# Cross-attention on one core: one weight quarter kept in SBUF, values loaded quad by quad, and one output product moved behind the values

## The chip, the cores and the metric

One core of one Trainium2 chip. The metric is the device time of one execution in microseconds (us), lower is better. The kernel before was timed in three runs.

## The reference

The inputs are `x` (8 batches x 256 rows x 1024), a context of the same shape that serves as keys and as values, a mask over the 256 context rows, two 1024 x 1024 weights and the layer norm's gamma and beta. All is fp32.

```python
xn = layernorm(x) * gamma + beta
Q = heads(xn @ Wq.T)                     # 32 heads of 32
scores = Q @ K.T / sqrt(32)              # K = V = heads(context)
attn = softmax(where(mask, scores, -inf)) @ V
out = x + merge(attn) @ Wout.T
```

## The kernel before

**Tiles.** The work goes by quads of four heads. A batch has 8 quads, so there are N = 64 quads, and one loop over n = 0..63 issues one slot each. Batch b's quads are 8b to 8b+7. The order on every engine is the order in which the program issues; no scheduler moves anything.

**One slot.** In slot n TensorE (PE) gets, in this order: the scores of quad n+1 (`sc`, L479), project steps of place 0, the values of quad n-2 (`pv`, L622, softmax times V), project steps of place 1, a query product or `make_q`, project steps of place 2. The other engines get the softmax of quad n+1: VectorE (DVE) adds the mask and takes the minimum (L515), ScalarE (ACT) takes the exponentials (L519), GpSimd (POOL) normalizes (L528), DVE transposes blocks into `pT` (L534), ACT puts a part aside in `pc` (`aside`, L540). The `tail` of a softmax, on SyncE's (SP's) queue, issues two pT-to-pT copies (L600), then the list `between` of loads, then two pc-to-pT copies (L604). For quads 0 to 7 and 57 to 62 the tail is put off to the next slot. A list `ahead` of loads is issued just before the tail. `pT` has three buffers, `pc` (pool `asp`) three.

**Query projection.** Batches 0 to 2 use whole weights (`make_q`). From batch 3 (`SPLIT`) on, the product of two 2x2 block matrices is made from seven half-size products, one per slot, in slots 8(b-1)+2 to 8(b-1)+8, in the order S1, S4, A11, S2, S3, A22, A12 (`Q_PRODUCTS`). Their PSUM bank is `ps_q` (one buffer, tag `pq`). Weight quarters and their sums lie in the tile `wq`, at the places of `W_AT`. Three of them share one SBUF tile, `ring`: T1 (for S1), B11 (for A11) and T3 (for S3) are kept in DRAM (`keep_wq`) and loaded back by halves of 512 KB (`load_ring`) in every batch. T4 lies in `wq` where B11 was before.

**Output projection.** Of a batch b it also takes seven products of four steps each (`PRODUCTS`: A11, A12, S2, S3, A22, S1, S4), spread over slots 8(b+1) to 8(b+1)+8 by the table `STEPS`, with (k0, k1, k2) steps at places 0, 1, 2. A step is one 128x512 matmul, two PE records. Their bank is `ps_o` (one buffer, tag `po`). A11 opens the bank in slot 8b+9 at place 0; `keep_p1` (ACT, L702) copies the result P1 aside; A12 then adds to the same bank from place 2 of that slot on, so that the bank holds P1 + A12 B21, which `store` (DVE, L736) adds to the residual `r` and sends out. `add_p1` (POOL, L727) adds P1 to the other three residual quarters. `ENDS` is the table of batch 6; batch 7 is written out after the loop.

**Values.** `load_v` loads V for a pair of quads (512 KB, two buffers) in the list `between` of every odd slot. `load_k` does so for keys in even slots.

**SP's queue** is one queue in order for all these DMAs: k, v, x, r, ring, output weights `wo`, the copies of pT and pc, the 64 KB copies `xnT<-xe` of a transposed x (`move_x`, L327), and the stores.

Of the kernel before, what the change touches and what calls it, by code (L numbers as in the profile page):

```python
# [46 lines left out]
F32 = mybir.dt.float32  # L47
# [4 lines left out]
P = 128  # L52
# [7 lines left out]
def xattn_kernel(  # L60
# [11 lines left out]
    nc = tc.nc  # L72
    B, S, D = x.shape
    T = mask.shape[2]
    HD = D // HEADS
# [6 lines left out]
    K = 32  # L82
    NA = P // K
    NI = T // (2 * K)
    assert NH == 4 and NS == 2 and NT == 2 and S == 256 and T == 256 and NA == 4
    NEG_SCALE = -1.0 / math.sqrt(HD)
    N = B * NQ

    const = ctx.enter_context(tc.tile_pool(name="const", bufs=1))
# [4 lines left out]
    vp = ctx.enter_context(tc.tile_pool(name="vp", bufs=2))  # L94
    atp = ctx.enter_context(tc.tile_pool(name="atp", bufs=3))
    ep = ctx.enter_context(tc.tile_pool(name="ep", bufs=4))
    ptp = ctx.enter_context(tc.tile_pool(name="ptp", bufs=3))
    asp = ctx.enter_context(tc.tile_pool(name="asp", bufs=3))
    up = ctx.enter_context(tc.tile_pool(name="up", bufs=1))
    sm = ctx.enter_context(tc.tile_pool(name="sm", bufs=8))  # L100
    dram = ctx.enter_context(tc.tile_pool(name="dram", bufs=1, space=bass.MemoryType.DRAM))
# [3 lines left out]
    ps_q = ctx.enter_context(tc.tile_pool(name="ps_q", bufs=1, space=PS))  # L105
    ps_o = ctx.enter_context(tc.tile_pool(name="ps_o", bufs=1, space=PS))

    NK = D // P // 2
    ring = const.tile([P, NK, NK, P], F32, tag="ring", name="ring")
# [13 lines left out]
    xs, ks, vs, rs = {}, {}, {}, {}  # L123
# [8 lines left out]
    def load_k(n):  # L132

        b, g = divmod(n, NQ)
        ks[n] = kp.tile([P, 2, T], F32, tag="k", name=f"k_{n}")
        nc.sync.dma_start(
            ks[n], kv[b, g // 2, :, : 2 * T].rearrange("p (g t) -> p g t", g=2)
        )

    def load_v(n):  # L140

        b, g = divmod(n, NQ)
        vs[n] = vp.tile([P, NI, 2 * P], F32, tag="v", name=f"v_{n}")
        nc.sync.dma_start(
            vs[n], kv[b, g // 2, :, 2 * T :].rearrange("p (i v) -> p i v", i=NI)
        )

    def load_res(b, s, h):
# [8 lines left out]
    sums_x = const.tile([P, 2, NK, NA, K], F32, tag="sx", name="sx")  # L157
    kept = {
        name: dram.tile([P, NK, NK * P], F32, tag=name, name=f"kept_{name}")
        for name in ("T1", "B11", "T3")  # L160
    }
    wo = const.tile([P, 7, NK, 512], F32, tag="wo", name="wo")
    B11, B21, B22, T1, T2, T3, T4 = range(7)
    B12 = T1

    def load_wq(o):
        nc.sync.dma_start(wq[:, o], wq_[o])
# [36 lines left out]
    for o in range(2, 5):  # L204
        load_wq(o)
    load_k(2)
    load_v(0)
    for o in range(5, 8):
        load_wq(o)

# [148 lines left out]
    def fold(o):  # L359
# [13 lines left out]
    SPLIT = 3  # L373
    SOON, LATE = 0, NK
    W_AT = {"B12": (SOON, 0), "B22": (SOON, NK), "B11": (LATE, 0), "B21": (LATE, NK),
            "T2": (SOON, 0), "T3": (SOON, 0), "T4": (LATE, 0)}

    def weights(name, o):

        if name == "ring":  # L380
            return ring[:, o]
        first, k = W_AT[name]
        return wq[:, first + o, ds(k, NK)]

# [20 lines left out]
    def load_ring(name, half):  # L405
# [1 line left out]
        nc.sync.dma_start(ring[:, pair].rearrange("p o c q -> p o (c q)"), kept[name][:, pair])  # L407

    Q_PRODUCTS = (
        ("S1", "ring", True), ("S4", "B22", False), ("A11", "ring", True), ("S2", "T2", False),  # L410
        ("S3", "ring", False), ("A22", "T4", False), ("A12", "B21", True),
    )

# [50 lines left out]
    mbs, scs, pTs, pvs, ats, pos = {}, {}, {}, {}, {}, {}  # L464
# [19 lines left out]
    def softmax(*args):  # L484
        for _ in softmax_parts(*args):
            pass
# [127 lines left out]
    def values(n):  # L614
        pvs[n] = [
            ps_v.tile([P, 2, NS, K], F32, tag="pv", name=f"pv_{n}_{r}") for r in range(2)
        ]
        pT = pTs.pop(n)
        for i in range(NI):
            for j in range(NH):  # L620
                for r in range(2):
                    nc.tensor.matmul(  # L622
                        pvs[n][r][j * HD : (j + 1) * HD],
                        vs[n - n % 2][ts(r, 2 * K), i, ds(n % 2 * P + j * HD, HD)],
                        pT[ts(r, 2 * K), :, i, j, :, :],
                        start=(i == 0), stop=(i == NI - 1),
                    )

    def copy_at(n):
# [4 lines left out]
        for r, pv in enumerate(pvs.pop(n)):  # L634
# [12 lines left out]
    PRODUCTS = (  # L647
        ("A11", B11, True), ("A12", B21, False), ("S2", T2, True), ("S3", T3, False),
        ("A22", T4, False), ("S1", T1, True), ("S4", B22, False),
    )  # L650

    STEPS = ((0, 0, 0), (4, 0, 3), (0, 1, 2), (0, 2, 2), (0, 2, 1), (0, 1, 2), (0, 0, 3), (0, 1, 2),
             (0, 2, 0))
    ENDS = ((0, 0, 2), (0, 0, 5), (0, 0, 5)) + ((0, 0, 4),) * 4 + ((0, 0, 0),)
    ENDS_TO = {2: (0, 0), 3: (0, 1), 4: (1, 1), 5: (1, 0), 6: (1, 1), 7: (0, 1)}
    assert all(sum(map(sum, one)) == len(PRODUCTS) * NK for one in (STEPS, ENDS))

    def operand(b, name):  # L660

        if name in ("S2", "S1"):
            return s2s[b]
        s, k = {"A11": (0, 0), "A12": (0, 1), "A21": (1, 0), "A22": (1, 1),
                "S3": (1, 0), "S4": (0, 1)}[name]
        return ats[b, k][:, :, s].rearrange("p c a k -> p c (a k)")
# [9 lines left out]
            operand(b, name)[:, c], operand(b, one)[:, c], operand(b, two)[:, c], op  # L676
        )

    s2s, p1s = {}, {}

    def product_steps(b, steps):
        for step in steps:
            p, c = divmod(step, NK)
            name, which, begins = PRODUCTS[p]
            po = pos.get(b)
            if b == B - 2 and name in ("A12", "S2"):

                begins = name == "A12"
                if begins and c == 0:
                    po_q[0] = ps_q.tile([P, 512], F32, tag="pq", name=f"po_{b}_{name}")  # L690
                po = po_q[0] if begins else po
            elif begins and c == 0:
                po = pos[b] = ps_o.tile([P, 512], F32, tag="po", name=f"po_{b}_{name}")
            nc.tensor.matmul(  # L694
                po, operand(b, name)[:, c], wo[:, which, c],
                start=begins and c == 0, stop=c == NK - 1,
                skip_group_check=not begins,
            )

    def keep_p1(b):  # L700
        p1s[b] = up.tile([P, 512], F32, tag="p1", name=f"p1_{b}")
        nc.scalar.copy(p1s[b], pos[b])  # L702


    po_q, ends_kept = [None], {}
# [76 lines left out]
    firsts = {NQ * (b - 1) + 2: b for b in range(SPLIT, B)}  # L782
# [55 lines left out]

    away, rings = {n: [] for n in range(N)}, {n: [] for n in range(N)}
    for n, name, half in (  # L840
        (9, "B11", 0), (10, "B11", 1), (15, "T1", 0), (16, "T1", 1), (17, "T3", 0), (19, "T3", 1),
    ):
        away[n].append(partial(keep_wq, name, half))
    for n, b in firsts.items():
        for slots, name in (((n - 3, n - 2), "T1"), ((n, n), "B11"), ((n + 2, n + 2), "T3")):
            if b > SPLIT or name != "T1":
                for half, slot in enumerate(slots):
                    rings[slot].append(partial(load_ring, name, half))
# [34 lines left out]
    steps, evacuations = {}, {n: [] for n in range(N + 1)}  # L883
    for b in range(B - 1):
        done, ends = 0, b == B - 2
        for i, counts in enumerate(ENDS if ends else STEPS):
            n = NQ * (b + 1) + i
            for place, k in enumerate(counts):
                steps.setdefault((n, place), []).append((b, range(done, done + k)))
                done += k  # L890
        for i, *what in (
            ((2, keep_p1), (3, take_po_q), *((i, copy_po, i) for i in range(3, 8))) if ends else
            ((1, keep_p1), (2, store, 0, 0), (3, take, 0, 1), (4, take, 1, 1), (6, store, 1, 0),
             (7, store, 1, 1), (8, store, 0, 1))
        ):
            evacuations[NQ * (b + 1) + i].append((what[0], b, *what[1:]))

    def project_steps(n, place):
        for one in steps.get((n, place), ()):
            product_steps(*one)  # L900


    for n in range(N):
        b, i = divmod(n - NQ, NQ)
        new_q = new_qs[n]
        between = []
        if n % 2 and n + 1 < N:
            between.append(partial(load_v, n + 1))
        elif n % 2 == 0 and n + 4 < N:
            between.append(partial(load_k, n + 4))  # L910
        ahead = rings[n]
        if n + 3 in firsts or n + 2 in firsts:
            between, ahead = between + ahead, []
        if b >= 0:
            if b == B - 2 and i - 1 in (5, 6):
                between.append(partial(send, b, *ENDS_TO[i - 1]))
# [18 lines left out]
        for what, one, *args in evacuations[n]:  # L935
            if one == B - 2:
                now.append(partial(what, one, *args))
            else:
                place = "p1" if what is keep_p1 else "soon" if i == 2 else 0 if i in (3, 4, 6) else 1
                hooks.setdefault(place, []).append(partial(what, one, *args))  # L940
        if n >= 2:
            values(n - 2)
# [20 lines left out]
        if n + 1 < N:  # L963
            softmax(n + 1, copies, ahead, between, hooks, fill)
        else:
            copy_at(n - 2)
            for load in between:
                load()
        if b >= 0 and i == 1:
            sum_at(b, "S2", *((slice(NK - 1, NK),) if b == B - 2 else ()))  # L970
# [42 lines left out]
        if N - NQ + 2 < n < N - 1:  # L1013

            c = n - (N - NQ + 3)
# [58 lines left out]
    for cols in (first_cols, last_cols):  # L1074
        po = to_c12[:, cols] if cols.start == 0 else ps_v.tile([P, P], F32, tag="pv", name="po_end")
# [43 lines left out]
```

## Time and profile before

| | |
|---|---|
| timed runs | 575.7 us median (574.19, 575.7, 576.84) |
| the profiled execution | span 577.6 us from first to last instruction; no other time is recorded for it |
| granted TensorE clock | 0.997 of full, mean |
| busy | PE 567.7 us (98%), DVE 458.6 (79%), ACT 412.1 (71%), POOL 404.7 (70%) |
| DMA | 117.98 MB, mean 204 GB/s |
| chain that ended last | PE 79%, POOL 8%, DVE 6%, issue 2%, DMA 2%, ACT 1% |

A slot lasts 7.5 us in the first batch and 8.5 to 9.4 us later. A row of the timeline gives the start, the duration, the engine, the line, the operation, the tiles, the shape, the number of merged instructions, and in brackets the idle time before it with what ended that. A PE row's duration overlaps the next row's start by some 0.07 us, so that costs are best read from one start to the next.

### The profile page before, as it was taken

The numbers are of one execution on the slowest core, as the hardware profiler recorded it, in microseconds if no ns is written. First come the engines' busy times: TensorE is split into PE (matmuls) and PEld (weight loads), VectorE is DVE, ScalarE is ACT, GpSimd is POOL, SyncE is SP. The second block draws the span as 40 slices with busy tenths as digits, with TensorE's granted clock in tenths as the row PEclk, the third lists the DMA queues.
The fourth block names the chain that finished last, engine by engine and source line by source line (L and its number), as shares of the span: only waits on it lengthen the run. The fifth ranks groups of instructions, "written<-read, shape, count | busy, mean of one in ns | idle before, by whom it ended". The sixth has DMA issues, their size and how long they took to land.

```text
span 577.6 us, 20001 instructions
## 1 busy us (share of the span) xinstructions
PE 567.7 (98%) x7162; PEld 392.2 (68%) x7162; DVE 458.6 (79%) x1695; ACT 412.1 (71%) x1425; POOL 404.7 (70%) x672
## 2 busy tenths in 40 slices
PE   8999998999999999899999999999999999999998
PEld 8788884666667777477776677667766777755444
DVE  6897887687878878678888888888877868879823
ACT  4688886677758857678577976779767866869820
POOL 1788998699896896665657775676656667448780
PEclk9999999999999999999999999999999999999999
DMA  8675778756778667776686767887658865436741
GB/s 312 224 211 184 218 240 209 244 172 196 196 229 271 215 188 219 225 222 202 181 247 181 233 196 201 237 257 217 186 160 254 239 192 147 130 112 182 214 154 74
DMA packets 47475, 117.98 MB, mean 204 GB/s; under 512 B 9104, under 2 KB 9872, under 8 KB 47376
## 3 DMA queue, kind: packets, MB, share of 16 engines
q1 hardware_dynamic: 47088, 116.69, 68.2%
q8 instruction: 57, 0.93, 0.7%
q14 instruction: 42, 0.34, 0.2%
q10 hardware_dynamic: 288, 0.01, 0.0%
HBM read 65.28 MB, written 11.53 MB: 133 GB/s over the span
## 4 chain that ended last, share of the span: by engine, by line
PE 79%; POOL 8%; DVE 6%; issue 2%; DMA 2%; ACT 1%; SPq 0%; DVEq 0%; POOLq 0%; ACTq 0%
PE po_S L694 17%; PE pq_A L440 16%; PE sc L479 10%; PE po_A L694 10%; PE pv L622 9%; PE pq_S L440 6%; POOL e L528 6%; PE pq L340 6%; DVE e L515 3%; PE po_end L761 2%; DVE pT L534 1%; PE po_last L761 1%; POOL wo L183 1%; DMA pT<-pT 1%; ACT e L519 1%
## 5 line engine op out<-in xcount | busy, mean ns | idle before, releaser
L528 POOL TENSOR_SCALAR e<-e,rden 128x256 f32<-128x256 f32 x512 | 237.0, 483 | 131.1 <-DVE rden L526 129.6
L519 ACT ACTIVATE e<-e,mn 128x256 f32<-128x256 f32 x512 | 254.0, 500 | 53.8 <-DVE mn L515 53.8
L534 DVE STREAM_TRANSPOSE pT<-e 128x512 f32<-128x512 f32 x256 | 180.7, 707 | 54.8 <-POOL e L528 43.8
L515 DVE CUSTOM_DVE_ANT_0 e<-sc,mb 128x256 f32<-128x256 f32 x512 | 185.9, 416 | 23.7 <-PE sc L479 23.2
L540 ACT COPY pc<-pT 128x512 f32<-128x512 f32 x128 | 79.0, 617 | 72.0 <-DVE pT L534 43.0
L519 ACT ACTIVATION_READ_ACCUMULATOR e<-e,mn 128x1 f32 x512 | 97.7, 191 | 0.0
L340 PE MATMUL pq<-xnT,wq 128*128 128x256 f32 (+1 forms) x368 | 84.1, 383 | 0.0
L340 PEld LDWEIGHTS pq<-xnT,wq 128*128 128x128 f32 x368 | 68.7, 190 | 14.3 <-issue 3.9
L479 PEld LDWEIGHTS sc<-k,qa 32*128 32x128 f32 x1024 | 46.2, 184 | 42.4 <-issue 20.6
L694 PE MATMUL po_S<-wo,at 128*128 128x512 f32 x152 | 74.5, 607 | 0.3 <-DVE r L736 0.3
L622 PE MATMUL pv<-pT,v 64*32 64x128 f32 x4096 | 74.3, 274 | 0.0
L622 PEld LDWEIGHTS pv<-pT,v 64*32 64x32 f32 x4096 | 56.9, 105 | 25.3 <-issue 11.9
L479 PE MATMUL sc<-k,qa 32*128 32x256 f32 x1024 | 73.6, 400 | 0.1
L694 PE MATMUL po_A<-wo,at 128*128 128x512 f32 x128 | 61.9, 616 | 4.2 <-issue 2.2
L694 PE MATMUL po_S<-wo,s 128*128 128x512 f32 x104 | 50.2, 606 | 0.3 <-DVE r L736 0.3
L515 DVE DVE_READ_ACCUMULATOR2_ANT mn<- 128x1 f32 x512 | 42.6, 83 | 0.0
L694 PEld LDWEIGHTS po_A<-wo,at 128*128 128x128 f32 x128 | 22.6, 190 | 29.2 <-issue 23.4
L526 DVE RECIPROCAL rden<-den 128x2 f32<-128x2 f32 x256 | 37.5, 146 | 5.9 <-ACT e L519 4.6
L440 PEld LDWEIGHTS pq_A<-xnT,wq 128*128 128x128 f32 x320 | 37.3, 192 | 4.8 <-issue 4.1
L694 PEld LDWEIGHTS po_S<-wo,at 128*128 128x128 f32 x152 | 25.6, 190 | 20.8 <-issue 19.3
L440 PE MATMUL pq_A<-xnT,wq 128*128 128x128 f32 x320 | 37.3, 275 | 0.0
L635 ACT COPY at<-pv 128x128 f32<-128x128 f32 x128 | 26.2, 253 | 8.7 <-PE pv L622 8.7
(95 smaller groups left out, 605.3 us busy)
## 6 DMA issues: line engine op xcount, KB each, us to landing
v<-in_kv_dram SPq DMA_DIRECT2D x32, 512.0 KB, 4.2
pT<-pT SPq DMA_DIRECT2D x128, 128.0 KB, 2.9
pT<-pc SPq DMA_DIRECT2D x128, 128.0 KB, 4.7
ring<-kept_T SPq DMA_DIRECT2D x18, 512.0 KB, 5.8
k<-in_kv_dram SPq DMA_DIRECT2D x32, 256.0 KB, 3.0
x<-in_x_dram SPq DMA_DIRECT2D x14, 512.0 KB, 5.5
r<-in_x_dram SPq DMA_DIRECT2D x28, 256.0 KB, 4.5
out_dram<-r SPq DMA_DIRECT2D x28, 256.0 KB, 3.9
```

The source lines that it names most:

```text
L340: nc.tensor.matmul(pqs[n], wq[:, o, c, :], xnTs[b](c), start=(c == 0), stop=(c == NC - 1),)
L440: nc.tensor.matmul(pqs[b][:, o, :], w[:, c], x_[:, c], start=begins and o + c == 0, stop=c == NK - 1, skip_group_check=True,)
L479: nc.tensor.matmul(scs[n][j][:, s, :], qa[r, n % NQ, ts(s, P)], ks[n - n % 2][r, n % 2, :], start=True, stop=True,)
L515: nc.vector.tensor_tensor_reduce(out=e[:, s, :], in0=pss[j][:, s, :], in1=mbs[n // NQ], scale=1.0, scalar=NO_SCORE, op0=ALU.add, op1=ALU.m ...
L519: nc.scalar.activation(e[:, s, :], e[:, s, :], AF.Exp, bias=mn[:, s : s + 1], scale=-1.0, accum_out=den[:, s : s + 1],)
L526: nc.vector.reciprocal(rden, dens[j])
L528: nc.gpsimd.tensor_scalar(es[j][:, s, :], es[j][:, s, :], rden[:, s : s + 1], 1.0, ALU.mult, ALU.mult,)
L534: nc.vector.transpose(pT[:, :, :, j, :, :].rearrange("p a i s k -> p (a i) s k"), es[j].rearrange("p s (b t) -> p b s t", t=K),)
L540: nc.scalar.copy(pc[:, :, ts(j, 2)], pT[:, 1, :, ts(j, 2)])
L622: nc.tensor.matmul(pvs[n][r][j * HD : (j + 1) * HD], vs[n - n % 2][ts(r, 2 * K), i, ds(n % 2 * P + j * HD, HD)], pT[ts(r, 2 * K), :, i, j, ...
L635: nc.scalar.copy(ats[b, k][:, c, :, ts(r, 2), :], pv.rearrange("p a s k -> p s a k"))
L694: nc.tensor.matmul(po, operand(b, name)[:, c], wo[:, which, c], start=begins and c == 0, stop=c == NK - 1, skip_group_check=not begins,)
```

## The change

1. T4 gets a tile of its own, `w_t4`. B11 therefore stays at its place in `wq`; it is not kept in DRAM and not loaded into `ring`. T3 is loaded right after S1, in slots n and n+1, where it was loaded in n+2. All ring loads go into `between`.
2. To make room, `load_v` loads one quad (256 KB, the two buffers now hold two quads), in slot n for the values of slot n+2, from the list `ahead`; the host lays V out so that a quad is contiguous. And `pc` has two buffers.
3. For the batches of `P1_ASIDE` (0, 2, 3, 4, 5) product A11 goes to the bank `ps_q` and is issued behind the values, at place 1, with A12 right behind it in `ps_o`. P1 is then not in A12's bank, so `add_p1` also runs for the quarter (0, 0), on POOL, ahead of its `store`; `keep_p1` and that `store` move behind the slot's exponentials.

```diff
-    asp = ctx.enter_context(tc.tile_pool(name="asp", bufs=3))
+    asp = ctx.enter_context(tc.tile_pool(name="asp", bufs=2))
...
-        vs[n] = vp.tile([P, NI, 2 * P], F32, tag="v", name=f"v_{n}")
+        vs[n] = vp.tile([P, NI, P], F32, tag="v", name=f"v_{n}")
...
-        for name in ("T1", "B11", "T3")
+        for name in ("T1", "T3")
     }
+    w_t4 = const.tile([P, NK, NK, P], F32, tag="t4", name="t4")
...
-    ("S1", "ring", True), ("S4", "B22", False), ("A11", "ring", True), ("S2", "T2", False),
+    ("S1", "ring", True), ("S4", "B22", False), ("A11", "B11", True), ("S2", "T2", False),
...
+    P1_ASIDE = (0, 2, 3, 4, 5)
     STEPS = ((0, 0, 0), (4, 0, 3), (0, 1, 2), (0, 2, 2), (0, 2, 1), (0, 1, 2), (0, 0, 3), (0, 1, 2),
              (0, 2, 0))
+    def steps_of(b):
+        if b == B - 2:
+            return ENDS
+        if b == 0:
+            return STEPS[:1] + ((0, 6, 0), (0, 2, 2)) + STEPS[3:]
+        return STEPS[:1] + ((0, 7, 0),) + STEPS[2:] if b in P1_ASIDE else STEPS
...
+            begins = begins or b in P1_ASIDE and name == "A12"
...
+            elif b in P1_ASIDE and name == "A11":
+                if c == 0:
+                    p1_pos[b] = ps_q.tile([P, 512], F32, tag="pq", name=f"po_{b}_{name}")
+                po = p1_pos[b]
...
-        nc.scalar.copy(p1s[b], pos[b])
+        nc.scalar.copy(p1s[b], p1_pos.get(b) or pos[b])
...
-        for slots, name in (((n - 3, n - 2), "T1"), ((n, n), "B11"), ((n + 2, n + 2), "T3")):
+        for slots, name in (
+            ((n - 3, n - 2), "T1"), ((n, n + 2 if b == SPLIT else n + 1), "T3"),
+        ):
...
-            ((1, keep_p1), (2, store, 0, 0), (3, take, 0, 1), (4, take, 1, 1), (6, store, 1, 0),
+            ((1, keep_p1), *(((2, add_p1, 0, 0),) if b in P1_ASIDE else ()), (2, store, 0, 0), (3, take, 0, 1), (4, take, 1, 1), (6, store, 1, 0),
...
-        if n % 2 and n + 1 < N:
-            between.append(partial(load_v, n + 1))
-        elif n % 2 == 0 and n + 4 < N:
+        if n % 2 == 0 and n + 4 < N:
             between.append(partial(load_k, n + 4))
-        ahead = rings[n]
+        ahead = [partial(load_v, n)] if n > 1 else []
+        between += rings[n]
```

## Prediction

> **What bounds the kernel now.** I read the page first (busy shares, chain), then TensorE's timeline row by row, then who waited for whom, then SP's timeline. From the page, the busy shares and the chain by engine:
>
> ```profile
> PE 567.7 (98%) x7162; PEld 392.2 (68%) x7162; DVE 458.6 (79%) x1695; ACT 412.1 (71%) x1425; POOL 404.7 (70%) x672
> PE 79%; POOL 8%; DVE 6%; issue 2%; DMA 2%; ACT 1%; SPq 0%; DVEq 0%; POOLq 0%; ACTq 0%
> ```
>
> From the waits of the PE engine (who, for whom: us in total, times, longest):
>
> ```profile
> PE po_A L694 <- issue: 2.2, 1, 2.2
> PE po_A L694 <- DMA wo<-in_woT_dram: 1.7, 1, 1.7
> PE po_S L694 <- DVE r L736: 0.6, 2, 0.3
> ```
>
> PE is the bound: 98% busy, and its longest waits behind the start come to 4.5 us in all. So the change can win only what stands between PE's rows, and lose wherever it puts a new wait there. Two stretches of PE's timeline matter. First slots 9 and 10, where batch 0's output products begin; then slots 25, 33, 41, 49, the same place for batches 2 to 5 (slot 25 shown):
>
> ```profile
> 88.10 1.15 PE L479 MATMUL sc<-k,qa 32*128 32x256 f32 x16
> 89.49 3.70 PE L694 MATMUL po_A<-wo,at 128*128 128x512 f32 x8 [0.24 <-ACT qa L349]
> 93.12 1.16 PE L622 MATMUL pv<-pT,v 64*32 64x128 f32 x64
> ...
> 98.06 1.13 PE L694 MATMUL po_A<-wo,at 128*128 128x512 f32 x2 [1.71 <-DMA wo<-in_woT_dram]
> ...
> 106.15 1.95 PE L694 MATMUL po_S<-wo,s 128*128 128x512 f32 x4 [0.29 <-DVE r L736]
> ...
> 230.77 1.15 PE L479 MATMUL sc<-k,qa 32*128 32x256 f32 x16
> 231.85 3.70 PE L694 MATMUL po_A<-wo,at 128*128 128x512 f32 x8
> 235.48 1.16 PE L622 MATMUL pv<-pT,v 64*32 64x128 f32 x64
> 236.56 2.84 PE L694 MATMUL po_A<-wo,at 128*128 128x512 f32 x6
> 239.34 1.15 PE L479 MATMUL sc<-k,qa 32*128 32x256 f32 x16
> ```
>
> The rows of slot 25 touch each other; those of slots 9 and 10 have holes. What fills these holes is on SP's timeline (first) and on the chain (second), which leaves PE here:
>
> ```profile
> 91.76 1.15 SPq L604 DMA_DIRECT2D pT<-pc  x2
> 92.96 5.58 SPq L327 DMA_DIRECT2D xnT<-xe  x6
> 98.65 1.16 SPq L600 DMA_DIRECT2D pT<-pT  x2
> 99.85 0.58 SPq L136 DMA_DIRECT2D k<-in_kv_dram  x1
> ```
>
> ```profile
> 100.48 4.74 DMA r<-in_x_dram
> 105.31 0.60 DVE r L736
> ```
>
> SP stands from 86.6 (the end of the `wo` issue) to 91.76 for the pT copies to land, then is held in the six xnT copies (1.8 us of it for `wo`), so the load of residual quarter (0,0) goes out at 100.48 and lands at 105.22; DVE waits 3.57 us for it, and PE's S2 starts at 106.15. From there PE has no wait until 149.76, where one of 0.29 us ends on DVE.
>
> **Part by part.** *B11 stays.* Two DMAs to DRAM and ten loads into `ring` of 512 KB go, 6.3 of 117.98 MB. PE waited for no ring load, so this gains nothing directly. The ring loads' waits on SP (12.1 us for pq_A, 5.4 for pq_S) mostly go too; behind them stood pT copies whose values come some 8 to 12 us after their issue (pT of quad 24 at 226.71, its values at 240.41). Taken at 0; were that cover gone, each such load would cost its longest wait, 2.3 us.
>
> *A11 behind the values, batches 2 to 5.* Slot 25 takes 239.34 - 230.77 = 8.57 us: scores 1.08, A11 3.63, values 1.08, A12 2.78. Ten records in a row elsewhere (510.88 to 515.37) take 4.49, eight take 3.63, so each more costs 0.43 and fourteen cost 6.21. The slot becomes 1.08 + 1.08 + 6.21 = 8.37: 0.2 us less, four times: -0.8 us. New waits in it: A11 needs the bank that DVE empties at 231.06 to 231.71, and would start at 232.93; S1 in slot 26 needs `keep_p1`, 0.56 us on ACT behind exponentials that end by 237.4, and would start at 242.2. Both are covered by over 1 us. DVE gains: its transposes there waited for the values (1.64 us at 308.65 in slot 33), which now come 3.6 us earlier. S2's bank is freed by `store`, now behind eight exponentials: in slot 34 DVE's first began at 313.61, eight take 2.8 and a reciprocal 0.2, the store 0.7, so 317.3 against S2 at 317.91. `add_p1` is one POOL row of 1.28 us per batch, five in all, set before `normalize`; in slot 34 POOL idled 2.21 us at that place. Taken at 0; without that cover 1.28 us a batch.
>
> *Two `pc` buffers.* ACT's copy for quad n+2 waits for the pc copies of quad n. Mostly they lie 7 us and more apart. In slots 8 and 9 they are 91.76 and 96.31, while pc copies took 6.0 to 8.2 us to land here: ACT may wait up to 3.6 us, and the exponentials behind it shift. DVE's wait of 3.57 us for `r` covers that; uncovered it would cost those 3.6.
>
> *Values by single quads.* 64 DMAs of 256 KB for 32 of 512; SP pays 0.58 us for each. SP has the time nearly everywhere: from the last DMA that stays ahead of v to the values lie 7 us or more, save in slot 10 (98.54 to 100.19) and where the values move forward: slot 25 (226.60 to 231.85: 5.2), slot 41 (367.86 to 371.84: 4.0) and slot 9. Nearest rows for the landing: k, also 256 KB, 3.0 us; v at 512 KB 4.2; both in a queue that is busy nine tenths in these stretches, where pc took up to 8.2. At 3.0 slots 25 and 41 cost nothing; at 5.8, the ring's median, 0.6 and 1.8. I take 3.0 there, the same size. On this the Trainium skill speaks against the change: "DMA: Bandwidth & Descriptors", Bandwidth and Rules for kernel authors, asks for batches of 1 MiB or more, and its Anatomy of one DMA section prices one at 2.0 us plus its bytes at 436 GB/s. As an estimate by that page, two quads cost 5.2 us for a pair's 3.2, where the rows give 6.0 for 4.2; with its 2.6 instead of 3.0 the sum below would end 0.4 us lower.
>
> *Slots 9 and 10.* By PE's work alone: scores 1.08, values 1.08, twelve records 5.35, scores 1.08, values 1.08, four records 1.82, `make_q` 3.62: S2 at 88.10 + 15.11 = 103.21 instead of 106.15, a gain of 2.94 at most. But three things stand in front. v of quad 7 goes out behind pc of quad 7 (ends 83.40, some 0.6 later now): landed by 87 at 3.0, by 92.3 at 8.2. I take 92.3, since it queues behind that very pc. Values then at 92.3, the next scores at 98.7, ready for values at 99.8. v of quad 8 goes out behind the six xnT copies, about 98.0, and lands at 101: values 101.0, A12 102.1, `make_q` 103.9, S2 107.5. And the residual: the DMAs ahead of it grow by one v quad, and those that held the xnT copies shrink by as much, so 105.22 stays; then comes `add_p1` 1.28, `store` 0.69 and three handovers, together 2.1: S2 not before 107.3. Both legs agree on 107.5, 1.3 later than now. PE has only the 0.29 at 149.76 to absorb it: +1.0 us. Uncertain from -2.9 (all three land early) to +6.5 (v of quad 8 takes the 8.2).
>
> **Sum.** -0.8 + 1.0 = +0.2 us on a span of 577.6. That span lies 1.9 above the median of the timed runs and above all three; the page does not say what lies around it. The profiled run also holds a 2.19 us "issue" wait at 243.75 that no queue explains, once in 64 slots; I neither gain nor lose it. "Runtime: NRT & Kernel Launch", Instruction fetch mechanics, says that refills of 256 instructions are mostly hidden, which would leave that row unexplained; by the page the sum stays. On the median: 575.7 + 0.2 = 575.9. A difference within 0.5% (2.9 us) is about what a measurement of this kernel cannot tell from none.
>
> **The rivals.** *No change, the forecast* (0.57): 575.9, own range 573.9 to 577.9.
>
> *The first batch's holes close* (0.18): wo no longer waited for, v of quad 7 in by 89.2, the residual in by some 103 since SP is held less. For: the v pair of 512 KB that stood ahead of `wo` becomes 256 KB, and the 1.71 us wait for `wo` falls in any case, as A12's later steps move to slot 10. Against: the residual's chain has `add_p1` added. Price -2.9 - 0.8 = -3.7: 572.0.
>
> *The single quads come late* (0.25), slower: in slots 10 and 41 PE stands for a v of 256 KB. With a landing time L, slot 10 costs L - 1.85 (98.0 + L + 6.5 against 106.15 + 0.29) and slot 41 L - 4.0; less the 0.8, that passes 2.9 us from L = 4.8 on. For: rows of 5.8 and 8.2 us in the same queue. Against: the 3.0 of k. At L = 5.3: +4.0, 579.7.
>
> **How the numbers follow.** The likeliest is 575.9. The range goes from the second case, 572.0, to nearly the third's price, 579.5; outside is about one fifth. The second case gives most of faster (0.18), the third slower (0.25), the rest is same (0.57).
>
> **What would show it.** In the trace after: ring loads x18 without B11, v x64; slots 25, 33, 41, 49 at 8.4 us with fourteen po_A records in a row; five more POOL adds r<-r,p of 1.28 us; in slots 9 and 10 values waiting for v, S2 near 107.5. Wrong if S2 starts before 105 or after 110, if values in slot 41 wait for v, or if PE shows waits on the bank `ps_q`.

## The result, and the profile after

The changed kernel takes 577.94 us (median of 20 runs, 576.63 to 581.42). The kernel before, run beside it, takes 575.92 (20 runs, 572.41 to 577.96). The ratio is 1.005, 95% interval 1.0037 to 1.0063: slower by 2.0 us by the medians, by 2.9 us (0.005 of 575.7) by the ratio. The profiled execution after has a span of 576.1 us, a time of 577.87 and a granted clock of 1.0 (3 of the 20 runs have that). So a time lies 1.8 us above its span. By that the span of before (577.6) belongs to a run of about 579.4, above all the timed ones. It holds the "issue" wait of slot 26, which cost 3.76 us there (PE's start of slot 27 less that of slot 26, against the same in the trace after) and which the trace after lacks. Without it, before's span is 573.8, and after is 2.3 us longer.

The page after, busy shares and the chain by engine:

```profile
PE 565.0 (98%) x7162; PEld 393.3 (68%) x7162; DVE 460.8 (80%) x1695; ACT 411.8 (71%) x1425; POOL 409.8 (71%) x677
PE 35%; DMA 1%; issue 0%; SPq 0%; DVE 0%
```

PE is as busy as before, and POOL has five instructions more. The chain's shares add up to 36% only: followed back from the end it stops in slot 41, at a load of v. The chain itself, in order of time (start, duration, what), shows why:

```profile
366.46 0.02 SPq L144
366.51 3.38 DMA v<-in_kv_dram
369.89 0.25 issue
370.14 1.26 PE pv L627 x63
```

The values of slot 41 stand for a v quad that took 3.38 us to land. PE's waits after (us in total, times, longest):

```profile
PE pv L627 <- DMA pT<-pT: 3.2, 1, 3.2
PE pv L627 <- ACT e L524: 2.0, 1, 2.0
PE busy L120 <- POOL ring masks.py:199: 1.3, 1, 1.3
PE pv L627 <- DMA v<-in_kv_dram: 0.5, 1, 0.5
```

All of the new waits are waits of values (`pv`). In PE's timeline the first two are in slots 9 and 10; slot 25 is below them:

```profile
88.26 1.15 PE L484 MATMUL sc<-k,qa 32*128 32x256 f32 x16
92.62 1.26 PE L627 MATMUL pv<-pT,v 64*32 64x128 f32 x64 [3.21 <-DMA pT<-pT]
93.81 5.42 PE L713 MATMUL po_A<-wo,at 128*128 128x512 f32 x12
99.15 1.15 PE L484 MATMUL sc<-k,qa 32*128 32x256 f32 x16
102.33 1.33 PE L627 MATMUL pv<-pT,v 64*32 64x128 f32 x64 [2.03 <-ACT e L524]
103.59 1.98 PE L713 MATMUL po_A<-wo,at 128*128 128x512 f32 x4
105.41 3.62 PE L343 MATMUL pq<-xnT,wq 128*128 128x256 f32 x16
...
232.62 1.15 PE L484 MATMUL sc<-k,qa 32*128 32x256 f32 x16
233.70 1.17 PE L627 MATMUL pv<-pT,v 64*32 64x128 f32 x64
234.79 6.28 PE L713 MATMUL po_A<-wo,at 128*128 128x512 f32 x14
241.00 1.15 PE L484 MATMUL sc<-k,qa 32*128 32x256 f32 x16
```

The names in the brackets are inferred and wrong here: of the transfers whose landing the trace has, the ones that ended just before were both v. (It lacks the landing of quad 7's pc copies, which went out 1.2 us ahead of its v.) SP's timeline gives the issues:

```profile
85.08 0.53 SPq L144 DMA_DIRECT2D v<-in_kv_dram  x1
85.66 1.15 SPq L605 DMA_DIRECT2D pT<-pT  x2
86.86 0.58 SPq L130 DMA_DIRECT2D x<-in_x_dram  x1
87.48 0.60 SPq L175 DMA_DIRECT2D wo<-in_woT_dram  x1
93.00 1.15 SPq L609 DMA_DIRECT2D pT<-pc  x2
94.20 4.83 SPq L330 DMA_DIRECT2D xnT<-xe  x6
99.13 0.53 SPq L144 DMA_DIRECT2D v<-in_kv_dram  x1
```

By the trace, v of quad 7 (issued 85.08) landed at 92.37 and its values began at 92.62; v of quad 8 (issued 99.13, behind the six xnT copies) landed at 102.19 and its values began at 102.33. S2 began at 108.86, 2.7 us later than before. The hole for `wo` at 98.06 is gone, and two larger ones are in its place.

By slots (from PE's start of a slot to that of the next, after minus before): +0.2 us ahead of slot 9; +2.5 over slots 9 and 10; -0.8 in slots 11 and 15, where before's run had small holes of its own; -0.2 in each of slots 25, 33 and 49; +0.5 in slot 41 (its -0.2 and a wait); +0.5 behind the last matmul. Sum +2.3, as above.

### The profile page after: what moved, and what is told of

Its sections match the earlier page's. It is cut to its first block, busy times and chain, and to the rows that moved or that the text cites. A ratio compares the mean times of both kernels' runs of the same rounds, so it can differ in the third digit from the quotient of the medians.

```text
span 576.1 us, 20131 instructions
## 1 busy us (share of the span) xinstructions
PE 565.0 (98%) x7162; PEld 393.3 (68%) x7162; DVE 460.8 (80%) x1695; ACT 411.8 (71%) x1425; POOL 409.8 (71%) x677
## 5 line engine op out<-in xcount | busy, mean ns | idle before, releaser
L713 PE MATMUL po_A<-wo,at 128*128 128x512 f32 x128 | 59.5, 606 | 0.0
L746 POOL TENSOR_TENSOR r<-r,p 128x512 f32<-128x512 f32 x23 | 29.3, 1276 | 7.4 <-DMA r<-in_x_dram 3.8
```

The source lines that it names most:

```text
L713: nc.tensor.matmul(po, operand(b, name)[:, c], wo[:, which, c], start=begins and c == 0, stop=c == NK - 1, skip_group_check=not begins,)
L746: nc.gpsimd.tensor_tensor(r, r, p1s[b], ALU.add)
```

## The experiments

The theory after the first look (T): the moved product is sound; the single quads of v come late. Rivals: the moved product costs (R1); two `pc` buffers hold ACT (R2); it is not v but the copies of pT and pc, or the queue as a whole, that come late (R3). All ratios are to the kernel before, five rounds each.

**One part alone.** `p3_alone` is before with the third part's lines only. `parts_1_2` is after with

```diff
-    P1_ASIDE = (0, 2, 3, 4, 5)
+    P1_ASIDE = ()
-        if b == 0:
+        if b == 0 and b in P1_ASIDE:
```

> Only the third part is made in the kernel before: A11 B11 of batches 0 and 2 to 5 behind the values, in the queries' bank, with add_p1; v by pairs, three pc buffers and B11 in the ring as before. Theory (the single quads of v come late, the moved product is sound): -0.2 us in each of slots 25, 33, 41, 49, no wait of values for v. In slot 9 values of quad 7 wait for the pc copies alone (issued 82.25, the first landed at 90.43): 91.2; S2 by TensorE's own work 105.3, by the residual's chain (r lands 105.22, add_p1 1.28, store 0.69) 107.5. Sum -0.8 + 0.8 = 0 (-0.5 to +0.5). Rival (the moved product itself costs the time): +2 to +3 us, as the whole change. Rival (the residual's chain does not bind): S2 at 105.3, sum -1.6.

> The change without its third part, all batches with A11 ahead of the values as before: B11 in SBUF, v by single quads, two pc buffers. Theory (late v and the two buffers cost, the moved product pays): in slot 9 A11 waits for ACT's copy of the queries (2.4 us with two buffers in the kernel before) and runs at half clock for some 4 us; values of quad 8 wait for v that goes out behind the six xnT copies (landing 101 to 102); S2 at 108 to 109; sum +2 to +4 us. Rival (the moved product costs the time): 0.

Measured: `p3_alone` 573.55 us (572.64 to 574.24) against 575.03, ratio 0.997 (0.9953 to 0.9987), faster than both kernels. `parts_1_2` 577.41 us, ratio 1.0044 (1.0027 to 1.0062). R1 falls: the moved product by itself is a gain of 1.5 us, and the other two parts by themselves a loss of 2 us. In `parts_1_2` slots 9 and 10 have a wait each, for ACT's copy of the queries and for v:

```profile
92.55 3.70 PE L713 MATMUL po_A<-wo,at 128*128 128x512 f32 x8 [3.18 <-ACT qa L352]
102.22 1.25 PE L627 MATMUL pv<-pT,v 64*32 64x128 f32 x64 [1.03 <-DMA v<-in_kv_dram]
```

PE's timeline of `p3_alone`, slots 9 and 10:

```profile
88.48 1.15 PE L479 MATMUL sc<-k,qa 32*128 32x256 f32 x16
90.20 1.62 PE L622 MATMUL pv<-pT,v 64*32 64x128 f32 x64 [0.58 <-DMA pT<-pc]
91.76 5.42 PE L708 MATMUL po_A<-wo,at 128*128 128x512 f32 x12
97.10 1.15 PE L479 MATMUL sc<-k,qa 32*128 32x256 f32 x16
98.18 1.16 PE L622 MATMUL pv<-pT,v 64*32 64x128 f32 x64
...
105.54 1.98 PE L708 MATMUL po_S<-wo,s 128*128 128x512 f32 x4 [0.84 <-DVE r L750]
```

Here v of quad 7 had come with that of quad 6, well before. Quad 7's pc copies, too, went out earlier (81.89; before 82.25, after 83.84) and landed at 90.07 and 90.56. The values wait 0.58 us where after they wait 3.21, nothing waits for `wo` since half of A12 now stands in slot 10 (a quarter before), and S2 starts 2 us before the expected 107.5: the residual landed at 103.36, not 105.22, as SP stood 0.47 us among the xnT copies where it had stood 1.78. Its chain still sets S2 (the 0.84).

A first kernel for parts 1 and 2, `b11_v_pc`, kept batch 0's own step table, so that there A11 stood behind the values in the old bank; P1 of batch 0 then also holds half of A12.

> The change without its third part: B11 in SBUF, v by single quads, two pc buffers; no batch has its A11 B11 moved. Theory: v of quad 7 lands at 92.4, covered by A11 ahead of it (values at 93.1); v of quad 8 goes out behind the six xnT copies, lands at 102.2, and values of quad 8 stand until 102.4, S2 near 108; no wait in slot 41, where A11 again stands ahead. Sum +1.0 to +2.0 us. Rival (the moved product costs the time): 0.

It took 579.65 us (six runs), ratio 1.0078 (1.005 to 1.0107), and answers another question than was asked; `parts_1_2` replaces it.

**Two `pc` buffers alone, and with the third part.**

```diff
-    asp = ctx.enter_context(tc.tile_pool(name="asp", bufs=3))
+    asp = ctx.enter_context(tc.tile_pool(name="asp", bufs=2))
```

> The kernel before with two pc buffers in the place of three, nothing else. Theory: ACT waits some 3.6 us once in slot 8 or 9, behind DVE's wait for the residual, and the time stays within 0.3 us. Rival (two buffers hold ACT and through it the values): +1 to +3.6 us.

> The third part alone with two pc buffers in the place of three; v by pairs, B11 in the ring. Theory (what the whole change loses against the third part alone comes of the v quads on SP and in the queues, and A11 in slot 9 no longer needs the bank that ACT's late copy of the queries frees): values of quad 7 at 90 to 91, S2 within 0.5 us of 105.5, ratio 0.997 to 0.999. Rival (the two buffers are what costs): values of quad 7 or the scores of quad 10 behind ACT, S2 at 107.5 or later, ratio 1.001 or above.

Measured: `pc_two` 575.54 us, ratio 1.0018 (0.9994 to 1.0042); `p3_pc_two` 574.66, ratio 0.9995 (0.9976 to 1.0014), 1.1 us above `p3_alone`. Neither interval settles it alone, but the trace of `pc_two` shows the wait. First ACT, then PE:

```profile
91.07 0.62 ACT L540 COPY pc<-pT 128x512 f32<-128x512 f32 x1 [3.23 <-DVE mn L515]
91.59 0.83 ACT L349 ACTIVATE qa<-pq,qa 128x256 f32<-128x256 f32 x2
```

```profile
92.11 5.23 PE L694 MATMUL po_A<-wo,at 128*128 128x512 f32 x8 [2.41 <-ACT qa L349]
97.28 1.16 PE L622 MATMUL pv<-pT,v 64*32 64x128 f32 x64
```

ACT's copy into `pc` stands for a buffer; behind it on ACT is the copy of the queries, which frees the bank that A11 opens; so PE stands 2.41 us. And eight `po_A` records take 5.23 us, not 3.70: in windows of 4 us the clock (the column before the DMA share) falls.

```profile
88.00:92.00 4.00, 1.70 (x19) 0.92 (x18) 3.82 (x16) 0.93 (x3) 3.68 (x7) 0.98 1.03 240
92.00:96.00 4.00, 3.89 (x6) 1.80 (x7) 1.82 (x12) 3.88 (x15) 3.91 (x6) 0.60 0.96 299
```

So R2 is real in its mechanism, which neither of my expectations for `pc_two` had. In `p3_pc_two` ACT stood as long (3.65 us), but A11 then came behind the values, and what PE waited for (1.20 us) was a pc copy; S2 came at 106.96, later than expected, in part since twelve `po_A` records took 6.33 us there (5.34 in `p3_alone`), again at a granted clock of 0.50 from 91.8 to 95.2. R2's price is some 1 us, not separable from none by these runs.

**Single quads alone.** Before, with v by single quads issued as after; B11 stays in the ring, three `pc` buffers.

```diff
-        if n % 2 and n + 1 < N:
-            between.append(partial(load_v, n + 1))
-        elif n % 2 == 0 and n + 4 < N:
+        if n % 2 == 0 and n + 4 < N:
...
+        if n > 1:
+            ahead = [partial(load_v, n)] + ahead
```

> The kernel before with v by single quads, each issued in its own slot ahead of that slot's pT copies, as after; B11 stays in the ring, three pc buffers, no product moved. Theory: the same late v of quad 8 as after, S2 near 108, sum +1.0 to +2.0 us. Rival (the moved product or the two buffers cost the time): 0.

Measured: 587.03 us (582.32 to 588.79), ratio 1.0198 (1.0163 to 1.0232): 12 us slower where 1 to 2 were expected. Two of PE's waits, then SP's longest wait here:

```profile
PE pv L624 <- ACT e L521: 5.4, 2, 3.0
...
PE pv L624 <- DMA v<-in_kv_dram: 1.3, 3, 0.9
```

```profile
SPq L606 <- DMA pT<-pT: 119.5, 63, 6.1
```

and the same wait of SP after:

```profile
SPq L609 <- DMA pT<-pT: 68.5, 61, 3.8
```

The values wait in slot 10 as after (2.96 us; v issued at 99.40 behind the xnT copies), but then also in slots 26, 40, 42, 48 and 50, and in slot 34 PE waits 0.86 us for a ring load, which it never did before. SP has fallen behind: it stands 119.5 us in all between a quad's pT copies and its pc copies (42.6 before, 68.5 after), so that v of quad 24 goes out at 240.54, in a queue where the pc copies ahead took 6.26 us and the pT copies behind it 5.98, and its values begin at 246.52 after a wait of 2.47. So T holds, but it priced one slot only. And the first part of the change is not worth nothing: with it, and with its ring loads moved behind the pT copies, single quads and two `pc` buffers cost 2 us (`parts_1_2`), without it single quads alone 12. Whether that is the ten ring loads less or their place on SP, these runs don't tell apart.

**v earlier in the change.** `v_ahead` puts v of quad 7 ahead of its slot's tail and every v ahead of the xnT copies; `v_swap` moves nothing but v of quads 7 and 8. `v_r_ahead` and `v_r_swap` add the residual quarter (0,0) behind v of quad 8. `v_swap`, against after:

```diff
+            if n == NQ:
+                while ahead:
+                    ahead.pop(0)()
             while tails:
...
         ahead = [partial(load_v, n)] if n > 1 else []
+        if n == NQ:
+            ahead += [partial(move_x, *args) for args in moves.pop(n - 1)]
...
-        for args in moves[n]:
+        for args in moves[n] if n != NQ - 1 else ():
```

In `v_ahead` the middle lines stand for every slot (`moves.get(n - 1, ())`), and the last loop is gone. The two others have `load_res(0, 0, 0)` appended ahead of `move_x` in slot 8.

> The whole change, with v of quad 7 issued ahead of that slot's pT copies and every other v ahead of the slot's xnT copies (these go out one place later). Theory: v lands by 80 (quad 7) and by 97 (quad 8); values of quad 7 then wait for their pc copies alone, 91.4 for 92.62, values of quad 8 for nothing, S2 at 107 by the residual's chain (105.4 by TensorE); the 0.5 us in slot 41 goes; sum -2.4 us against the whole change, +0.5 against the kernel before. Rival (the pT and pc copies, or ACT with two buffers, hold the values and not v): no gain, +2 to +3 against the kernel before.

> As v_ahead, and the load of the residual quarter (0,0) goes out right behind v of quad 8, ahead of the six xnT copies. Theory: r lands by 98, the residual's chain no longer binds, S2 at 105.4 by TensorE: -1.6 us against v_ahead, about -1 against the kernel before. Rival (the residual's chain is not what binds S2, or the earlier load delays the copies by as much): no gain over v_ahead.

> The whole change; only two transfers change places: v of quad 7 goes ahead of that slot's pT copies, and v of quad 8 ahead of the six xnT copies of slot 7 (all other moves stay where they are). Theory (v itself is late): values of quad 7 at 92.0 for 92.6, held by pc alone, values of quad 8 right after the scores at 99.6 for 102.3, S2 at 108.0 by the residual's chain; -0.9 us against the whole change. Rival (SP's issues and the queue as a whole are late, v is only the last of several that land at 91 to 92.5): values of quad 7 at 92.0 or later since the pc copies now stand 0.6 behind, S2 no earlier than 108.8, no gain.

> As v_swap, with the load of residual quarter (0,0) right behind v of quad 8, ahead of the six xnT copies. Theory: the residual's chain no longer sets S2, which starts at 106.1 by TensorE: -2.7 us against the whole change. Rival (the residual is not what sets it): as v_swap.

Measured: `v_ahead` 577.88 us (ratio 1.0056, 1.0038 to 1.0075) and `v_r_ahead` 577.88 (1.0046, 1.0026 to 1.0065): no gain, as R3 had it. But in these two ten xnT copies stood ahead of quad 7's tail, whose pc copies went out at 86.06 (`v_r_ahead`: 85.08), 2.2 and 1.2 us later than after; the values of quad 7 began at 93.47 and 93.70. They moved one late transfer ahead by making another late. The wait in slot 41 did go. `v_swap` does it cleanly: 576.59 us, ratio 1.0028 (1.0011 to 1.0045), some 1.3 us better than after, though the two intervals overlap a little. Its PE timeline:

```profile
91.48 1.72 PE L630 MATMUL pv<-pT,v 64*32 64x128 f32 x64 [2.15 <-issue]
93.39 6.84 PE L716 MATMUL po_A<-wo,at 128*128 128x512 f32 x12 [0.19 <-ACT qa L352]
100.16 1.15 PE L484 MATMUL sc<-k,qa 32*128 32x256 f32 x16
101.23 1.16 PE L630 MATMUL pv<-pT,v 64*32 64x128 f32 x64
```

v of quad 7 landed at 83.77, v of quad 8 was issued at 93.67. The second wait is gone (values at 101.23, right behind the scores), and S2 begins at 107.59 (T: 108.0; R3: no earlier than 108.8). The first wait is only shortened to 2.15 us: the second of quad 7's pc copies landed at 91.88. So T holds for quad 8 and R3 for the rest of quad 7. That S2 came so near T's 108.0 is luck: T had it held by the residual, but it waited for nothing, and the twelve `po_A` records ahead of it took 6.77 us from start to start where after they take 5.34, at a granted clock of 0.50 from 92.9 to 96.3. The clock hid 1.4 us of the gain in this profile. `v_r_swap` at 577.4 (1.0041, 1.0022 to 1.0059) gained nothing over `v_swap`: S2 waits for the residual in neither, and in its profile the values of quad 7 began at 92.84 and S2 at 108.49.

**The residual earlier beside the third part.**

```diff
+        if n == NQ - 1:
+            load_res(0, 0, 0)
         for args in moves[n]:
```

> The third part alone, with the load of residual quarter (0,0) ahead of the six xnT copies of slot 7. Theory: the 0.84 us in which S2 waits for the residual there goes, S2 at 104.7, sum -0.8 us against the third part alone, ratio to the kernel before 0.9955. Rival (the 0.6 us that this load takes on SP and in the queues delays the pT copies by as much): no gain, ratio 0.997 or above.

573.03 us (572.56 to 575.4), ratio 0.997 (0.995 to 0.999): not told apart from `p3_alone`. In its profile (of its slowest run, 575.4 us) S2 no longer waits for `r`, but quad 7's pc copies went out at 83.06, and its values wait 1.44 and 0.30 us.

**Batch 0 as before in the change** (`P1_ASIDE = (2, 3, 4, 5)`, with the second line of `parts_1_2`).

> The whole change with batch 0 left as before (A11 ahead of the values there); batches 2 to 5 have A11 behind the values. Theory: slots 9 and 10 as in parts 1 and 2 alone (A11 covers the late v of quad 7, S2 at 107.8 for 108.9 in the whole change), slots 25, 33, 49 0.2 us shorter, values of slot 41 0.5 late: 0.5 to 1 us faster than the whole change, ratio 1.0035. Rival (batch 0's move pays here too, as in the third part alone): 1 us slower than the whole change.

578.42 us, ratio 1.0047 (1.0025 to 1.0068): not told apart from the change. The PE waits show what took the place of the wait for v:

```profile
PE po_A L713 <- ACT qa L352: 3.2, 1, 3.2
```

With A11 first again, A11 waits for ACT as in `pc_two`, longer still. Whichever comes first in slot 9, it waits for something that comes at 91 to 92.6. Eight `po_A` records then take 5.33 us, not 3.63, at a granted clock of 0.50 from 93.0 to 96.4, so this run does not show what the order is worth at full clock.

## Why the prediction was right and wrong

The range (572.0 to 579.5) held the time; the forecast of 575.9 was 2.0 us low. That range reached from one rival's price to nearly the other's, so holding the time says little. What happened is nearest to the third rival, single quads that come late, at 2.0 to 2.9 us for its 2.9 to 4.0. Its places were half right: it named slots 10 and 41, and slot 9 was the first. Its reason was not: it rested on landings of 4.8 us and more, and v took 3.07 us in slot 10 and 3.38 in slot 41. One of the prediction's own signs of being wrong came true, the wait of the values in slot 41.

*B11 stays, 0.* PE waited for no ring load before, and that was read rightly. But `v_single` is 12 us slower than before and `parts_1_2` only 2: the zero may hold for the removal alone, which no run tried, but not beside single quads. The two should have been priced together, as queue room given and taken.

*A11 behind the values, -0.2 in each of four slots.* Right: -0.19, -0.20, -0.20 in slots 25, 33 and 49. Fourteen records took 6.28 us (forecast 6.21). No wait on `ps_q`, on `keep_p1` or on `store` appeared. `add_p1` is hidden (POOL, all 23 at a mean of 1.28 us). In slot 41 the -0.2 and a wait for v made +0.5.

*Two `pc` buffers, 0.* A wait on ACT of this size was foreseen (up to 3.6 us; 3.88 after), but one quad too late and under the wrong cover. It was put at 96.31, behind the pc copies issued at 91.76; it came ahead of ACT's copy at 91.07 (`pc_two`) and 91.48 (after), behind the pc copies that go out at 82 to 84. DVE's wait for `r` ends at 105.3, long after; what stood behind ACT was the copy of the queries, whose bank A11 opens, at 89.5. I named what is hidden and not what is queued behind the waiting instruction. In the change itself this wait does not show, since v is later still.

*Single quads, a landing of 3.0 us.* Too short over the whole run. The page after, DMA issues (count, KB each, median us to landing):

```profile
v<-in_kv_dram SPq DMA_DIRECT2D x64, 256.0 KB, 4.2
```

That is the 4.2 us of the 512 KB pairs before (medians over the 39 of 64 and 14 of 32 landings that the traces have). The pairs and k went out behind a quad's pT copies, single quads go out right behind pc copies, so size and place changed together; the row of k (3.0) had the size alone. But where a single quad's landing entered the sum, 3.0 was nearly right (3.07 and 3.38). What was off there is when v goes out: 1.1 us later in slot 10, and in slot 41 only 3.1 us, not 4.0, ahead of the place where the values could begin.

*Slots 9 and 10.* The order of events was right, each a little later: v of quad 7 landed at 92.37 (92.3); v of quad 8 issued at 99.13 (98.0), as the pc copies ahead waited until 93.00, landed at 102.19 (101.0); S2 at 108.86 (107.5). The residual's leg was ready at about 107.8 (107.3) and did not bind. A loss of 2.7 in place of 1.3 (0.16 of it came in with the start of slot 9); of it 0.8 was given back instead of 0.29.

*The first rival* (the holes close, 572.0). One of its three conditions came true, the `wo` wait is gone; v of quad 7 did not land by 89.2, nor the residual by 103 (105.58). The third part without the other two comes nearest to this rival: residual at 103.36, 573.55 us, a gain of 1.5 us for its 3.7. I set its price on the whole change and did not see that one part earns and another spends.

*The clock* was in no term. The mean granted clock was 1.0 in 3 of the 20 runs after, and 0.994 to 0.997 in 17; by groups their medians are 577.0 us (1.0, 3 runs), 577.81 (0.996 to 0.997, 12) and 579.86 (0.994, 5). Of 23 runs of before beside `p3_alone`, 2 lay at 0.997, and of the 12 of `p3_alone` none. As an estimate from the three runs at 1.0, 0.9 of the 2.0 us is the clock's (577.94 less 577.0), and the rest mostly the waits'.

*Smaller slips.* `make_q` was counted at its duration, 3.62 us; from start to start it is 3.45. The third rival's L - 1.85 is L - 1.94 by its own numbers. A v of 2.6 us would have lowered the sum by 0.2, not 0.4, since the residual's leg stood at 107.3. The price of the Trainium skill, "DMA: Bandwidth & Descriptors", Anatomy of one DMA, is a fit for DMAs that GpSimd issues, where these are SyncE's. The queue was not busy nine tenths in slots 25 and 41: the DMA share is 0.76 at 224 to 232 and 0.68 at 366 to 372. The example of pT copies 8 to 12 us ahead of their values (226.71 to 240.41) is 13.7 us. None of these moves the forecast by more than 0.2 us.

The parts do not add up: 0.997 times 1.0044 is 1.0014, and the whole is 1.005, some 2 us more. The profiles of `p3_alone`, `parts_1_2` and after, all three at a clock of 1.0, show where. Against before, slots 9 and 10 together are 1.0 us shorter, 1.5 longer and 2.5 longer, and slot 41 is 0.2 shorter, the same and 0.5 longer. With A11 first, the late v of quad 7 is covered by A11 and its wait (it lands at 92.46 in `parts_1_2`, and its values begin at 96.18); with the values first nothing covers it. So the third part gains 1.5 us beside pairs, and nothing beside single quads (1.005 against 1.0044). The wait of slot 26 in before's profile stays unexplained.

## What to carry to other kernels

Price what is taken from a loaded queue and what is put into it as one sum: here fewer ring loads seemed worth nothing and single quads little, and without the one the other cost 12 us. For a transfer, ask first when its queue will send it, and for its landing look at rows with the same place in the queue, not only the same size. Before moving work behind a load, check that the same change does not make the load late. And when one engine waits for a buffer, list what is behind it on that engine, above all the copy that frees a PSUM bank.

## What the runs showed of the hardware

A wait of PE may cost more than its length. After the 2.19 us wait at 243.75 in before's profile the granted clock was 0.50 from 244 to 247 (windows of 1 us), and 32 `pq_S` records took 4.54 us, where the next 32 (at 255.59) took 3.73. In `pc_two` a wait of 2.41 us had the same effect, in `p3_pc_two` one of 1.20 with 0.30 right behind it. After the 3.21 us wait in the profile of after the clock stayed at 1.0. So the length of the wait alone does not decide.

The traces show what goes with it. Every stretch of half clock ahead of the last matmul lasts 3.41 us (6.83 in `v_ahead`), and where the same profile has another, that begins a whole number of 3.41 us later: in `pc_two` the first ends at 95.23 and the one behind the last matmul begins at 576.51, 141 such steps on. Counted on this grid, the clock fell after each of the ten steps, over all the profiles here, in which PE stood idle for 1.85 us or more (`pc_two`, 88.41 to 91.82: 2.12), after none with 1.16 or less, and after three of the seven in between. The 3.21 us wait of after fell on an edge of the grid (counted back from the clock's fall at 575.80), so that neither step was idle enough. The two steps in the profile of after (behind the length, PE's busy time; the clock stands before the DMA share):

```profile
87.69:91.10 3.41, 1.72 (x19) 0.94 (x18) 3.23 (x10) 0.00 (x0) 1.97 (x5) 1.00 1.01 264
91.10:94.51 3.41, 1.89 (x66) 1.49 (x67) 2.83 (x15) 3.03 (x10) 3.41 (x4) 1.00 1.03 305
```

One stretch loses 1.7 us of clock, 0.003 of a run: a mean clock of 0.997 is one stretch, 0.994 two. `p3_alone`, whose longest wait within the loop is 0.84 us, shows none in its 12 runs (clock 0.999 or 1.0) and is also the steadiest kernel (1.6 us between its extremes, before's 23 runs 5.6).

The Trainium skill, "TensorE: Matmul & The Clock Gate", section What's actually happening, has a free-running window of 3.4 us and a half rate as the other of two states. The stretches of 0.50, their length of 3.41 us and the grid agree with that. Its section Why this matters for your kernels asks for no gaps over some 3 us; here 1.20 was enough once, and 3.21 was not.
